# A fixed lead in the scheduler's order for the work beside a selective scan

## The chip, the cores and the metric

The kernel runs on one core of a Trainium2 chip. The metric is the device time of one execution in microseconds (us); the time given is the median of three runs. Engines are named as in the profile: PE is TensorE's matmul, PEld its weight load, DVE is VectorE, ACT ScalarE, POOL GpSimd, SP SyncE.

## What is computed

Eight images of 64 channels and 64 x 64 pixels go through four layers one after the other, all in float32:

```
x = layer0(x)   # softmax attention of all 4096 pixels over 4096, then a 3x3 depthwise and a 1x1 convolution
x = layer1(x)   # norm, then two blocks of 8x8 window attention (8 heads) and an MLP with gelu
x = layer2(x)   # a dynamic 3x3 filter made from x, leaky relu, a 1x9 convolution
x = layer3(x)   # norm, projection, depthwise conv, selective scan in 4 directions, gate, then a
                # multi-scale depthwise stage (max pools, 3x3 convolutions, gelu)
```

The selective scan is the recurrence of layer 3, for 128 channels and 16 states along 4096 positions, in four directions:

```
h = h * exp(dt_t[..., None] * A) + dt_t[..., None] * B_t[:, :, None, :] * u_t[..., None]
y_t = einsum('bkcn,bkn->bkc', h, C_t)
```

## The kernel before

Images are worked on in four pairs p = 0 to 3; the two images of a pair share the 128 partitions. The work of a pair has three parts:

- **the front** (`front(p)`): layers 0 to 2 and the sources of the scan. `layer0` is the attention: 8 column chunks by 32 row tiles by 2 images of a score matmul (L1324), an exp on ACT (L1330) and a weighing matmul (L1316), then a convolution. `layer1` is a norm, two rounds of eight window rows (L1453, L1470, L1471, L1483, L1494) and of an MLP (L1552 to L1560). `layer2` weighs nine taps on DVE (L1619) and sums them on PE (L1625, L1637). `scan_sources` normalises, projects, convolves (L1275, L1277) and stores x2, xc, xt and zs in device memory; its last instructions are the 16 z (L1693), eight for each image.
- **the scans** (`scans(p)`): 2 images x 4 directions x 8 chunks of 512 positions make 64 units of 8 steps, so 512 steps a pair and 2048 in all. A step takes two pairs of states. `fetch` loads B and C rows three and two steps ahead (four buffers each, SP's queue), `products` makes dt·u·B on POOL (L1809, eight buffers `v`), `step` makes two exps on ACT (L1831), two scans on DVE (L1834), copies the ends for the next chunk (L1838) and multiplies by C on POOL or DVE (L1842), `sums` folds the result into the accumulator `yd` on PE (L1854). Once a unit there are `load`, `inputs`, `spread` for the next and `gather` for the last one; after the last direction (the order is 1, 3, 0, 2, and the last runs from chunk 7 down to 0) `gather` stores the chunk of `ys` (L1873). The next chunk of a direction needs the carries of the one before.
- **the back** (`back(p)`): from chunk 7 down to 0 it loads x2, and for both images y (from `ys`, L1890) and z, normalises and gates (L1894, L1895: 16 `u`), projects and adds; then the multi-scale stage, and the store of the output.

`begin` runs front 0 alone. Then there are four sections. Section p traces the scans of pair p, and beside them, one after the other, back(p-1) and front(p+1); the last section has back(2), spread over more steps, and near its end back(3), which the program calls `late`. The generators yield an estimated cost, and the loop of `scans` pulls work from them in proportion to the steps, so that it is used up LEAD = 24 steps before the section's end.

The program gives every instruction a number in the order in which it is traced (a counter that goes up by one for each). The scheduler then makes each engine's queue: it goes through the program in a model of time, and gives a free engine, among the instructions of that engine which are ready, the one with the lowest number. So an instruction of the front that has fallen behind has a lower number than the scan instructions now ready, and one that is ahead has a higher. On the chip each engine works its queue in that fixed order.

The front and the back take their large tiles from three slabs (`self.slabs`, three buffers of one tag), in the order of the trace; the front's and the scans' PSUM banks are apart (`pf`, `ps`), save while the front is alone and in the last section after its back stage has been traced, when `bank` alternates between them.

Of the kernel before, what the change touches and what calls it, by code (L numbers as in the profile page):

```python
# [25 lines left out]
NTD = L // TD  # L26
GRP = 2
LEAD = 24
TC = 1024
NTC = L // TC  # L30
SLAB = 66 * 66
# [206 lines left out]
class _Net:  # L238
# [764 lines left out]
    def piece(t, k, c):  # L1003

        if k % 2 == 0:
            return t.rearrange("p (h w) -> p h w", w=64)[:, c * TC // 64 : (c + 1) * TC // 64, :]
        return t.rearrange("p (h w) -> p w h", w=64)[:, c * TC // 64 : (c + 1) * TC // 64, :]

    def scan_inputs(self, XC, unit, pools):
# [6 lines left out]
        nbc = 2 * NST  # L1016
        px = ps.tile([P, TC], F32, name="px", tag="pr")
        for h in range(TC // CH):
            nc.tensor.matmul(
# [5 lines left out]
            )  # L1025
        xd = wk.tile([nbc + RNK, TC], F32, name="xd", tag="xd", bufs=1)
        nc.scalar.activation(xd, px[0 : nbc + RNK], AF.Copy)
# [132 lines left out]
class _Direct:  # L1160
# [552 lines left out]
    def scans(self, p, beside, cost):  # L1713

        self.units = []
        for im in range(2):
            out = self.memory("ys")
            self.kept["y", 2 * p + im] = out  # L1720
            for nth, k in enumerate((1, 3, 0, 2)):
                order = range(NTD) if k < 2 else range(NTD - 1, -1, -1)
                self.units += [dict(image=2 * p + im, k=k, c=c, at=at, nth=nth, out=out) for at, c in enumerate(order)]
        self.load(self.units[0])
        self.inputs(self.units[0])
        self.spread(self.units[0])
        n = 8 * len(self.units)

        late = self.back(p) if p == B // 2 - 1 else None
        steps = [{} for _ in range(n)]  # L1730
        done = 0
        for i in range(-3, n):
            if i + 3 < n:
                self.fetch(i + 3, steps[i + 3], 0)
            if 0 <= i + 2 < n:
                self.fetch(i + 2, steps[i + 2], 1)
                self.products(i + 2, steps[i + 2])
            if i >= 0:
                self.step(i, steps[i])
                for j in self.DUE[i % 8]:  # L1740
                    if i + j >= 0:
                        self.sums(i + j, steps[i + j], steps[i]["w"])
                if i % 8 == 2 and i > 8:
                    self.gather(self.units[i // 8 - 1])
                if p == B // 2 - 1 and done >= cost:
                    self.turn = max(self.turn, 0)
                while done < cost * (i + 1) / (n - LEAD):
                    done += next(beside, cost)
            if late and i >= n - 8 * (NTD - 1) and i % 8 in (3, 5, 7):
                next(late)  # L1750
            if i >= 0 and i % 8 < 3 and i // 8 + 1 < len(self.units):
                (self.load, self.inputs, self.spread)[i % 8](self.units[i // 8 + 1])
        for i in (n - 2, n - 1):
            self.sums(i, steps[i])
        self.gather(self.units[-1])
        self.run(beside)
        if late:
            self.run(late)
# [285 lines left out]
```

## Time and profile before

| | |
|---|---|
| median of three runs | 11726.25 us (11724.63 to 11733.27) |
| the profiled execution | 11724.67 us, its span 11722.8 us |
| granted TensorE clock, mean | 0.896 |
| busy: PE, DVE, ACT, POOL | 9682.2, 8416.8, 7078.9, 6924.2 us |
| scans on DVE (L1834, the four groups) | 2602.0 + 1922.7 + 352.3 + 261.9 us, 4096 of them |
| attention exps on ACT (L1330) | 2048, 589 ns each |
| DMA | 1577.06 MB, mean 135 GB/s |

The profile is of one execution. Its page has the busy time of each engine and the busy tenths in 40 equal slices. A table of stretches gives for each stretch of time, in us from the span's start, its length, the busy time of each engine with the number of its instructions, the granted clock, the DMA engines' share and the GB/s; for one source line alone it gives those instructions only. Busy PE time is modelled, since matmuls are pipelined.

The front's stages can be told by their lines: front 0 has its attention from 45 to 579 us and its last z at 1547; front 1 has its first exp at 1579, its last at 2600, its last z at 4024; front 2 has 4437, 5388 and 6790; front 3 has 7200, 8149 and 9562. The last scan starts at 11602.8, and the output's last stores follow.

### The profile page before, as it was taken

How to read it: one execution, taken by the hardware profiler on the slowest of the kernel's cores; microseconds unless marked ns; L12 is line 12 of the kernel's file. 1: busy time of each engine (PE TensorE's matmuls, PEld its weight loads, DVE VectorE, ACT ScalarE, POOL GpSimd, SP SyncE). 2: the span in 40 equal slices, each digit the busy share in tenths (PEclk: the TensorE clock that was granted, in tenths of full speed). 3: DMA queues.
4: the chain of work that ended last, by engine and by line, in shares of the span. 5: the costliest groups of instructions: out<-in, count | busy, mean ns of one | idle time of the engine just before them, and what ended most of it. 6: DMA issues, size and time to landing. Idle time of an engine off the chain costs nothing. (4 is left out here: it accounts for less than half of the span.)

```text
span 11722.8 us, 161838 instructions
## 1 busy us (share of the span) xinstructions
PE 9682.2 (83%) x55454; PEld 3278.2 (28%) x55454; DVE 8416.8 (72%) x9856; ACT 7078.9 (60%) x16513; POOL 6924.2 (59%) x3799
## 2 busy tenths in 40 slices
PE   9987899998879779998888969999888976655556
PEld 2244332223332222222442213222333221111111
DVE  0033368887777685778777775878778669989998
ACT  5545367766664756776665665776666465555554
POOL 0000058876665565777555574777556558778994
PEclk9998989999999889999999879999998977877677
DMA  0000055553444554555333463555334356556663
GB/s 21 1 2 2 27 164 176 172 174 118 128 124 123 168 165 128 167 169 164 103 113 110 140 201 102 171 166 173 120 106 129 109 172 196 171 177 200 205 205 120
DMA packets 779781, 1577.06 MB, mean 135 GB/s; under 512 B 89280, under 2 KB 89408, under 8 KB 778176
## 3 DMA queue, kind: packets, MB, share of 16 engines
q1 hardware_dynamic: 736320, 1443.18, 40.6%
q10 hardware_dynamic: 42624, 123.44, 3.7%
q8 instruction: 438, 7.18, 0.2%
q14 instruction: 399, 3.27, 0.1%
HBM read 1197.16 MB, written 100.66 MB: 111 GB/s over the span
## 5 line engine op out<-in xcount | busy, mean ns | idle before, releaser
L1809 POOL TENSOR_TENSOR vd<-B,du 128x1024 f32<-128x1024 f32 x2048 | 4801.7, 2363 | 2896.0 <-DMA B<-rows 1732.7
L1842 POOL TENSOR_TENSOR vd<-hd,C 128x512 f32<-128x512 f32 x1737 | 2210.8, 1278 | 1765.4 <-DVE hd L1834 1719.2
L1854 PE MATMUL yd<-vd,pack 128*64 128x512 f32 x8192 | 2684.9, 691 | 602.0 <-POOL vd L1842 501.5
L1831 ACT ACTIVATE dad<-du,As 128x512 f32<-128x512 f32 x4096 | 2719.1, 682 | 635.5 <-DVE vd L1842 412.5
L1834 DVE TENSOR_TENSOR_SCAN dad<-dad,carry,vd 128x512 f32<-128x512 f32 x2064 | 2602.0, 1275 | 228.4 <-ACT dad L1831 224.8
L1834 DVE TENSOR_TENSOR_SCAN hd<-dad,carry,vd 128x512 f32<-128x512 f32 x1520 | 1922.7, 1266 | 347.5 <-ACT dad L1831 298.2
L1842 DVE TENSOR_TENSOR vd<-dad,C 128x512 f32<-128x512 f32 x2359 | 1559.6, 673 | 167.9 <-ACT carry L1838 128.7
L1324 PE MATMUL s<-X 64*128 64x512 f32 x4096 | 1542.2, 644 | 74.9 <-ACT e L1330 68.9
L1330 ACT ACTIVATE e<-s 128x512 f32<-128x512 f32 x2048 | 1197.3, 589 | 468.1 <-PE s L1324 467.8
L1854 PEld LDWEIGHTS yd<-vd,pack 128*64 128x64 f32 x8192 | 651.9, 151 | 2292.6 <-issue 1169.1
L1316 PE MATMUL po<-e,VT 128*64 128x512 f32 x4096 | 1264.5, 620 | 9.5 <-ACT e L1330 8.7
L1838 ACT ACTIVATE carry<-dad 128x1 f32<-128x1 f32 x2063 | 345.8, 169 | 903.4 <-DVE dad L1834 804.4
L1324 PEld LDWEIGHTS s<-X 64*128 64x128 f32 x4096 | 422.2, 186 | 1181.4 <-issue 831.3
L1838 ACT ACTIVATE carry<-hd 128x1 f32<-128x1 f32 x1521 | 303.1, 200 | 678.4 <-DVE hd L1834 669.8
L1483 PE MATMUL w_av<-wide,vals 64*32 64x64 f32 x16384 | 502.6, 227 | 127.3 <-DVE w_oc L1512 74.2
L1483 PEld LDWEIGHTS w_av<-wide,vals 64*32 64x32 f32 x16384 | 416.7, 113 | 258.9 <-issue 138.6
L1316 PEld LDWEIGHTS po<-e,VT 128*64 128x64 f32 x4096 | 250.5, 135 | 841.0 <-issue 565.7
L1471 ACT ACTIVATE wide<-wide 128x512 f32<-128x512 f32 x512 | 310.9, 628 | 287.0 <-DVE wide L1470 287.0
L1494 PE MATMUL w_av<-wide,each 64*32 64x128 f32 x8192 | 474.4, 284 | 8.4 <-issue 8.3
L1243 PE MATMUL pv<-n_sq,pack 128*128 128x512 f32 x576 | 354.7, 700 | 139.6 <-ACT n_sq L1241 127.0
L1771 PE MATMUL pdd<-xs,xdt 128*128 128x512 f32 x512 | 343.7, 758 | 122.3 <-DVE hd L1834 64.2
L1330 ACT ACTIVATION_READ_ACCUMULATOR e<-s 128x1 f32 x2048 | 406.7, 199 | 0.0
(258 smaller groups left out, 10839.1 us busy)
## 6 DMA issues: line engine op xcount, KB each, us to landing
B<-rows SPq DMA_DIRECT2D x2048, 256.0 KB, 3.6
C<-rows SPq DMA_DIRECT2D x2048, 256.0 KB, 3.5
du<-du SPq DMA_DIRECT2D x384, 512.0 KB, 5.5
du<-du ACTq DMA_DIRECT2D x128, 512.0 KB, 5.2
xs<-xt SPq DMA_DIRECT2D x128, 256.0 KB, 3.7
xs<-xc SPq DMA_DIRECT2D x128, 256.0 KB, 3.8
xc<-xcv ACTq DMA_DIRECT2D x64, 256.0 KB, 2.0
xt<-XT ACTq DMA_DIRECT2D x32, 512.0 KB, 5.9
```

Source lines behind the costliest of these rows:

```text
L1243: nc.tensor.matmul(pv, lhsT=avg, rhs=sq, start=True, stop=True)
L1316: nc.tensor.matmul(po[half[im]], lhsT=VT[:, t, half[im]], rhs=es[im], start=(t == 0), stop=(t == 31))
L1324: nc.tensor.matmul(ss[im], lhsT=at(half[im], t), rhs=X[half[im], jc * CH : (jc + 1) * CH], start=True, stop=True)
L1330: nc.scalar.activation(e, ss[im], AF.Exp, scale=C**-0.5, accum_out=parts[:, im, t, jc : jc + 1])
L1483: nc.tensor.matmul(self.av[rows, 0, x % 4 + j], lhsT=net.vals[half[im], x + j, 4 * g + h], rhs=es[g][half[im], j, h], tile_position=(64 * ...
L1494: nc.tensor.matmul(self.av[rows, 1, x % 4 : x % 4 + 2], lhsT=net.each[half[im], 32 - HD - HD * h : 64 - HD - HD * h], rhs=es[g][half[im], ...
L1809: self.nc.gpsimd.tensor_tensor(v, self.twice(st["B"]), self.units[i // 8]["du"][:, :, 1], ALU.mult)
L1831: nc.scalar.activation(da, u["du"][:, j, 0], AF.Exp, scale=net.As[:, k, n : n + 1])
L1834: nc.vector.tensor_tensor_scan(along(to), along(da), along(v[:, j]), first, ALU.mult, ALU.add)
L1838: nc.scalar.activation(self.carries[:, n : n + 1], ends, AF.Copy)
L1842: m = engine.tensor_tensor(v[:, j], hs[j], CC, ALU.mult)
L1854: m = nc.tensor.matmul(u["y"][self.HALF[j]], lhsT=w["fold"], rhs=st["v"][:, j], start=(i % 8 == 0), stop=(i % 8 == 7))
```

## The change

The block in which `scans` pulls work of the front and the back is put under `high_priority(offset=AHEAD)`. This sets the counter back by 600 for the instructions traced inside, and sets it to its old value afterwards, so that these instructions no longer advance the counter. No instruction is added, removed or changed; `begin`, the rest of `beside` after the loop and `late` keep their numbers.

```
+AHEAD = 600
...
                 while done < cost * (i + 1) / (n - LEAD):
-                    done += next(beside, cost)
+                    with self.tc.high_priority(offset=AHEAD):
+                        done += next(beside, cost)
```

## The prediction, made before the result was known

> **What bounds the kernel now.** I read the page's busy line and slices first, then a table of stretches cut at the front's own stages (first and last exp of L1330, last z of L1693), then the same stretches for the scan instruction L1834 alone, which counts scan steps (two scans to a step, 2048 steps in all).
>
> From the page, busy tenths in 40 slices (293 us each):
>
> ```profile
> PE   9987899998879779998888969999888976655556
> DVE  0033368887777685778777775878778669989998
> PEclk9998989999999889999999879999998977877677
> ```
>
> TensorE is high for three quarters of the span, VectorE only at the end. Stretches, all engines: the first front's attention and its rest, alone; the turn between two sections; the third front's attention beside scans; two stretches after the last front, with no front or back work:
>
> ```profile
> 45.00:579.00 534.00, 534.00 (x2042) 130.44 (x2039) 4.85 (x7) 322.95 (x1023) 0.00 (x0) 1.00 0.00 1
> 579.00:1547.00 968.00, 797.45 (x9146) 383.59 (x9144) 350.57 (x570) 433.45 (x697) 0.00 (x0) 0.90 0.06 20
> ...
> 4024.00:4437.00 413.00, 321.09 (x766) 105.82 (x767) 321.55 (x373) 219.68 (x479) 265.38 (x146) 0.86 0.52 158
> 4437.00:5388.00 951.00, 922.46 (x3014) 253.66 (x3011) 715.30 (x757) 686.62 (x1955) 691.82 (x373) 0.99 0.54 159
> ...
> 10368.00:10600.00 232.00, 125.25 (x266) 24.15 (x266) 199.66 (x212) 113.86 (x264) 192.11 (x105) 0.70 0.63 191
> 10600.00:11385.00 785.00, 445.97 (x1026) 97.11 (x1024) 746.61 (x797) 406.95 (x992) 737.45 (x400) 0.71 0.67 204
> ```
>
> The columns after the length are PE, PEld, DVE, ACT, POOL. Attention is TensorE's (534 of 534 us alone, 922 of 951 with scans); the scans alone are VectorE's (747 of 785). The same for L1834 alone, from the second front's attention on (columns: length, DVE busy with the number of scans, clock, DMA share, GB/s):
>
> ```profile
> 1579.00:2600.00 1021.00, 626.22 (x510) 0.99 0.60 176
> 2600.00:4024.00 1424.00, 577.57 (x470) 0.91 0.44 132
> 4024.00:4437.00 413.00, 188.56 (x154) 0.86 0.52 158
> 4437.00:5388.00 951.00, 525.57 (x429) 0.99 0.54 159
> 5388.00:6791.00 1403.00, 543.05 (x441) 0.90 0.41 126
> ...
> 9562.00:10368.00 806.00, 469.94 (x385) 0.78 0.59 179
> 10368.00:10600.00 232.00, 148.79 (x122) 0.70 0.63 191
> 10600.00:11385.00 785.00, 549.56 (x454) 0.71 0.67 204
> 11385.00:11622.00 237.00, 125.59 (x103) 0.83 0.58 178
> ```
>
> After the last front's end at 9562 there are 385 + 122 + 454 + 103 = 1064 scans left, 532 steps: that front ended with the scans at step 1516 of 2048. The table gives two prices of a scan step. Alone it costs 232/61 = 3.80 us, and 785/227 = 3.46 us once the scans have the front's PSUM banks too. Beside a front it costs far less: the second front's attention carried 255 steps in 1021 us and the third's 214.5 in 951, so 70 us for 40.5 steps, **1.73 us a step**; for whole fronts (2445 us with 490, 2354 with 435) it is 91/55 = 1.65. So a step moved from beside a front to a place without one costs about 2 us. Who has the right of way today is seen where the third front's attention starts (L1834 alone, 50 us each):
>
> ```profile
> 4350.00:4400.00 50.00, 10.29 (x9) 1.00 0.26 83
> 4400.00:4450.00 50.00, 4.91 (x4) 0.83 0.24 85
> 4450.00:4500.00 50.00, 2.66 (x3) 1.00 0.03 9
> 4500.00:4550.00 50.00, 32.27 (x28) 1.00 0.67 189
> ```
>
> The back stage had fallen behind the scans, so the front's instructions had the older numbers; they took TensorE, the scans fell to 1.5 steps in 50 us, and at 4500 the two were level and went on in step (14 steps). A front that is behind already goes first. What the offset adds is that it goes first until it is ahead.
>
> **The change, part by part.** Nothing is added or removed but order. One scan step issues 2 exps, 2 scans, 2 products with C (and up to 2 carries, 1.75 on average), 1 product with B, 2 matmul calls, 2 fetches: 12.75; a unit of 8 steps adds 12 to 13 (load, two matmuls, four activations, a product, row store, spread, gather), so 14.3 instructions a step. The counter is put back after the block, so front instructions do not advance it: 600 numbers are 600/14.3 = **42 scan steps**. Where front and scans compete at level today, they will compete with the front 42 steps ahead; the pattern inside a section is the same, shifted. What changes is at the ends.
>
> (1) The first section. The second front cannot start earlier: it waits for the first one's slabs and pools, as today (its first exp is at 1579, 32 us after the first front's last z). It then takes TensorE until it leads by 42 steps, as at 4400 to 4500. Its attention carries some 213 steps instead of 255: 42 x 1.73 = **-73 us** until that front's end. Bounds: 42 x 3.8 = -160 if a step cost there what it costs alone, 0 if it cost nothing.
>
> (2) The last front. It ends with the scans at about step 1474 instead of 1516. Those 42 steps still have to be done, without a front, VectorE-bound, at 3.80 us: **+160 us** (at 3.46, +145). The third back stage beside them moves forward by the same 42 steps, so its own cost stays.
>
> (3) The two turns between. The back stage needs the three slabs of the front that is ending, then, from the last chunk down, what the scans of the second image's last direction store. Today the front's last z is at 4024 with the scans at step 493 of 512, when five of the eight chunks are stored; the sixteen u (L1895) of the stage come between 4087 and 4283, at step 554. Forty-two steps earlier the front ends at step 451, chunk 7 is complete at 456 and chunk 0 only at 512: the stage is held to one chunk in 8 steps. To step 512 that is 61 steps, as many as today from z to the last u (259 us, 4.25 a step), and behind the last store come its load and one chunk's norms (4 us and 196/8 = 25 us): some 35 us longer. The 8 steps done more in the turn are missing in the next attention (8 x 1.73 = -14 us). **+20 us each, +40** for both; bounds: 0 (the stage is not held), +90 (nothing given back). VectorE and ACT have room for it there (322 and 220 of 413 us).
>
> (4) Queues. SyncE's queue carries B and C for the scans, and the moved back stage issues its loads of y into it, now just behind the stores of the same rows: store 3.5 us and load 4.3 us to landing. B and C run three steps (over 11 us) ahead, which hides 7.8 us; uncovered it would be 8 x 7.8 = 62 us a section. I take 0. ACT's queue carries xc, xt, zs and the spread of the last images: same order within the front, 0. POOL has no front work; it only starves when the scans do, as at 4400, 0 beyond (1).
>
> Sum: -73 + 160 + 40 = **+127 us**. The profiled execution took 11724.67 us (span 11722.8), 1.6 under the median of 11726.25: 11852, say **11850**.
>
> Two rules of the Trainium skill against this sum. In the stretches without a front the granted clock was 0.70 and 0.71, against 0.99 in attention, so longer such stretches mean slower matmuls; yet VectorE is the bound there and TensorE is idle 46% of the time, so I add nothing. The skill ("TensorE: Matmul & The Clock Gate", Part 1) says that the array's clock is gated until activity releases it; were TensorE on the path there, that rule would add something, which no run here prices. And its "Perfetto Trace Analysis" (Identifying the Most-Contended Engine) says that busy matmul time is no measure of headroom and weight-load time should be used: by that, 254 of 951 us, attention has room, a step costs nothing in it, term (1) is 0 and the sum +200. The 70 us for 40.5 steps decide here.
>
> **The rivals.**
> - *The fronts themselves get shorter* (the other side). Layer 2 and the sources run level with the scans today: 3556 to 4024, 468 us, against 306 us for the first front alone (1241 to 1547). The excess, some 160 us a section, 480 for three, is partly front instructions queueing behind scan ones. If precedence gave back half while the scans filled the same holes: -240 + 127, **11610**. It decides from 127/480, a quarter, on. For it: ACT and DVE are each under 70% there, so there are holes. Against: where the front was behind and already first, it went no faster than its own chain.
> - *The back stage's loads block SyncE's queue*: the uncovered price of (4) in three sections, +187 us at most, half of it likely: **11945**. For it: y's load already waits for ys 8 times today. It decides if B's wait grows in the turns.
> - *The offset does nothing*: if in the scheduler's model the fronts are rarely ready when a scan instruction is, order hardly moves: **11726**. Against: the level stretch after 4500 is a contest.
>
> **How the numbers follow.** Forecast 0.55 (own range 11750 to 11925: (1) at -120, (2) at +145, (3) at 0 for the low end; -50, +160 and +90 for the high one), SyncE 0.17, nothing 0.06, shorter fronts 0.22, spread over 11500 to 11720. A measurement of this kernel tells about 0.2%, 23 us, from no change. Range 11600 to 11980: it leaves out the better half of the shorter fronts and the worst of SyncE. Faster 0.22, same 0.06, slower 0.72.
>
> **What would show it.** Right: the second front's attention starts with 100 to 150 us of almost no scans and takes about 950 us; the last z comes near 9530 with some 1475 steps done; L1834 then has about 1146 instructions left instead of 1064; the turns show the back stage beginning before the section's last scan step and paced by stores. Wrong: the fronts' non-attention stretches shrink well below 1400 us with as many scans in them; or the step count at the last z stays near 1516.

## The result and the profile after

The changed kernel takes 12749.2 us (median of four runs, 12740.08 to 12754.33) against 11725.44 for the kernel before beside it: ratio 1.087, interval 1.085 to 1.0885. The forecast of 11850 had the side right and the size far too small, outside its range. The profiled execution has a span of 12738.3 us and a mean clock of 0.865 (0.896 before). In this program the lines from 1748 on are two higher than in the one before, those from 29 to 1747 one higher: the scan is L1836, the window scores L1454.

The page of the kernel after, busy times and tenths (now 318 us a slice):

```profile
PE 10599.9 (83%) x55454; PEld 3559.2 (28%) x55454; DVE 8425.7 (66%) x9856; ACT 7093.4 (56%) x16505; POOL 6929.5 (54%) x3799
...
PE   9977999988989789998898869998988975665556
...
DVE  0133367776566757776656685778566668988998
...
PEclk9998999988888889998878889999888887777777
```

VectorE, ScalarE and GpSimd have the busy time they had. TensorE has 918 us more with the same 55454 matmuls, nearly the 1016 by which the span grew, and its clock is lower in the middle of each front. Stretches of the kernel after, all engines: turn, third front's attention, then 232 and 785 us from the last front's end:

```profile
4232.00:4659.00 427.00, 323.61 (x756) 103.39 (x756) 321.75 (x369) 220.09 (x485) 276.09 (x155) 0.85 0.52 158
4659.00:5697.00 1038.00, 976.26 (x3010) 267.67 (x3010) 706.20 (x743) 690.19 (x1957) 689.73 (x373) 0.95 0.49 144
...
10419.00:10651.00 232.00, 138.24 (x322) 31.20 (x318) 199.94 (x213) 124.21 (x288) 201.28 (x115) 0.76 0.61 184
10651.00:11436.00 785.00, 499.52 (x1132) 126.17 (x1132) 703.24 (x752) 429.19 (x955) 621.82 (x330) 0.77 0.60 181
```

The same kernel, scan instructions alone. First the 100 us from the second front's first exp, then its attention, its windows and MLP, its layer 2 and sources, the turn, the third front's attention and its windows and MLP, and everything behind the last z:

```profile
1567.00:1617.00 50.00, 4.66 (x4) 0.99 0.27 82
1617.00:1667.00 50.00, 8.25 (x7) 1.00 0.17 42
```
```profile
1567.00:2583.00 1016.00, 529.57 (x436) 0.97 0.52 152
2583.00:3678.00 1095.00, 395.96 (x321) 0.85 0.36 106
3678.00:4232.00 554.00, 183.92 (x149) 0.86 0.41 126
4232.00:4659.00 427.00, 189.78 (x155) 0.85 0.52 158
4659.00:5697.00 1038.00, 514.99 (x423) 0.95 0.49 144
5697.00:6781.00 1084.00, 379.49 (x308) 0.82 0.34 102
...
10419.00:12738.30 2319.30, 1395.13 (x1144) 0.76 0.60 182
```

The lead is there, and of the size worked out: the attention starts with 100 us of almost no scans, and 1144 scans are left behind the last z (1146 forecast). What had not been expected is the length of the fronts. The ledger below is cut at the first and last exp of each attention, the last addition of the MLP, the last z, and the end; each entry is us / scan steps.

| part | before | after | us more |
|---|---|---|---|
| to the second front's first exp | 1579 / 4 | 1567 / 0 | -12 |
| attentions beside scans | 1021 / 254, 951 / 214, 949 / 214 | 1016 / 218, 1038 / 212, 1038 / 212 | -6, 87, 89 |
| windows and MLP | 903 / 158, 871 / 149, 878 / 149 | 1095 / 160, 1084 / 153, 1079 / 153 | 192, 213, 201 |
| layer 2 and sources | 521 / 77, 532 / 71, 535 / 71 | 554 / 74, 557 / 69, 540 / 69 | 33, 25, 5 |
| turns | 413 / 77, 409 / 78 | 427 / 78, 424 / 78 | 14, 15 |
| behind the last z | 2161 / 532 | 2319 / 572 | 158 |

The tail behind the last z costs what was forecast (+160); the second front's attention gained almost nothing of the 73 us. Windows and MLP cost 606 us more with as many scan steps in them, and 587 of that lies between the first and the last projection of the window rows (`w_pp`, with the first of the two MLP rounds between them). The third front's rows, cut there, before and then after:

```profile
5595.00:6154.00 559.00, 471.99 (x7866) 240.52 (x7864) 420.74 (x554) 364.25 (x751) 304.08 (x171) 0.95 0.37 110
```
```profile
5907.00:6675.00 768.00, 700.39 (x7886) 322.69 (x7886) 432.45 (x564) 369.42 (x772) 321.07 (x179) 0.79 0.28 83
```

The same work, 209 us longer: VectorE, ScalarE and GpSimd do nearly as much, TensorE is busy for 228 us more at 0.79 of the clock instead of 0.95. The timeline of TensorE shows why. Start, length of the run of matmuls, line and tiles; before, then after, in the same part of a window row:

```profile
5657.37 1.51 PE L1453 MATMUL w_s<-wide,w_kk 32*64 32x256 f32 x20
...
5663.43 1.09 PE L1453 MATMUL w_s<-wide,w_kk 32*64 32x256 f32 x14
5664.45 0.43 PE L1483 MATMUL w_av<-wide,vals 64*32 64x64 f32 x16
5664.69 0.40 PE L1494 MATMUL w_av<-wide,each 64*32 64x128 f32 x8
5664.91 0.40 PE L1483 MATMUL w_av<-wide,vals 64*32 64x64 f32 x16
5665.14 0.40 PE L1494 MATMUL w_av<-wide,each 64*32 64x128 f32 x8
```
```profile
6053.10 0.64 PE L1454 MATMUL w_s<-wide,w_kk 32*64 32x256 f32 x2
6053.67 0.30 PE L1484 MATMUL w_av<-wide,vals 64*32 64x64 f32 x2
6053.90 0.64 PE L1454 MATMUL w_s<-wide,w_kk 32*64 32x256 f32 x2
6054.47 0.30 PE L1484 MATMUL w_av<-wide,vals 64*32 64x64 f32 x2
6054.69 0.64 PE L1454 MATMUL w_s<-wide,w_kk 32*64 32x256 f32 x2
```

Before, scores (`w_s`, 32 rows of the array) and weighings (`w_av`, 64 rows) go mostly in large groups. After, in many stretches, they alternate two by two (a float32 matmul of the code stands in the trace as two: 4096 scores for the code's 2048, so it is one matmul of each kind in turn), and each round of four matmuls takes 0.80 us (6053.10 to 6053.90). At the pace of the rows before, two scores are 2 x 0.06 us (20 in 1.51 us, the last one 0.37) and two weighings 2 x 0.015 (16 started in 0.24): 0.15 us. Over the whole trace, in order of start, TensorE goes directly from one of the two kinds to the other 342 times before and 1252 times after. Two groups of the page of the kernel after belong to it: the scores, busy for 798.5 us (344.0 before), and VectorE's idle time ahead of the bias, 449.9 us (109.8 before), nearly all of it put down to a weighing:

```profile
L1454 PE MATMUL w_s<-wide,w_kk 32*64 32x256 f32 x4096 | 798.5, 456 | 28.4 <-DVE wide L1471 26.5
...
L1471 DVE TENSOR_TENSOR wide<-w_s,bias 128x512 f32<-128x512 f32 x512 | 328.4, 683 | 449.9 <-PE w_av L1495 379.1
```

This is not the front against the scans, it is the front against itself. The counter is put back after each block that is pulled, so the next block starts from a number that is higher only by what the scans issued in between. A scan step issues some 14 instructions, a block of the window attention some 60 (8 scores, 48 weighings, two biases, two exps). By the trace of the kernel before, the third front issues about 34 a scan step in windows and MLP (5019 in 148.5 steps, matmuls counted as in the code) and 7 in its attention (1539 in 214.5). So in the window rows several successive blocks of the front share a range of numbers, and a score of a later block can have the number of an earlier block's weighing; in the attention, by this count, only blocks pulled at one step do. That gives the theory: *the front's own order is lost (1), and the lead has little to do with it*. The rival: *the lead itself does it (2)*, since scans and front meet at other places.

### The profile page after: what moved, and what is told of

It is laid out like the page before. It is cut to its first block, busy times and chain, and to the rows that moved or that the text cites. A ratio compares the mean times of both kernels' runs of the same rounds, so it can differ in the third digit from the quotient of the medians.

```text
span 12738.3 us, 161752 instructions
## 1 busy us (share of the span) xinstructions
PE 10599.9 (83%) x55454; PEld 3559.2 (28%) x55454; DVE 8425.7 (66%) x9856; ACT 7093.4 (56%) x16505; POOL 6929.5 (54%) x3799
## 5 line engine op out<-in xcount | busy, mean ns | idle before, releaser
L1811 POOL TENSOR_TENSOR vd<-B,du 128x1024 f32<-128x1024 f32 x2048 | 4796.7, 2360 | 3562.2 <-DMA B<-rows 1829.8
L1856 PE MATMUL yd<-vd,pack 128*64 128x512 f32 x8192 | 2896.7, 703 | 686.9 <-POOL vd L1844 612.7
L1836 DVE TENSOR_TENSOR_SCAN dad<-dad,carry,vd 128x512 f32<-128x512 f32 x2064 | 2600.5, 1275 | 85.2 <-ACT dad L1833 82.5
L1836 DVE TENSOR_TENSOR_SCAN hd<-dad,carry,vd 128x512 f32<-128x512 f32 x1520 | 1925.0, 1267 | 160.5 <-ACT dad L1833 120.0
L1325 PE MATMUL s<-X 64*128 64x512 f32 x4096 | 1511.1, 654 | 164.9 <-ACT e L1331 136.4
L1856 PEld LDWEIGHTS yd<-vd,pack 128*64 128x64 f32 x8192 | 677.7, 154 | 2554.1 <-issue 1198.6
L1317 PE MATMUL po<-e,VT 128*64 128x512 f32 x4096 | 1326.0, 641 | 15.0 <-ACT e L1331 12.8
L1454 PE MATMUL w_s<-wide,w_kk 32*64 32x256 f32 x4096 | 798.5, 456 | 28.4 <-DVE wide L1471 26.5
L1484 PE MATMUL w_av<-wide,vals 64*32 64x64 f32 x16384 | 669.3, 241 | 46.1 <-ACT wide L1472 22.9
L1471 DVE TENSOR_TENSOR wide<-w_s,bias 128x512 f32<-128x512 f32 x512 | 328.4, 683 | 449.9 <-PE w_av L1495 379.1
L1484 PEld LDWEIGHTS w_av<-wide,vals 64*32 64x32 f32 x16384 | 498.0, 121 | 404.5 <-issue 307.7
L1495 PE MATMUL w_av<-wide,each 64*32 64x128 f32 x8192 | 582.7, 308 | 2.1 <-issue 2.0
```

Of the source, the lines that this page charges most:

```text
L1317: nc.tensor.matmul(po[half[im]], lhsT=VT[:, t, half[im]], rhs=es[im], start=(t == 0), stop=(t == 31))
L1325: nc.tensor.matmul(ss[im], lhsT=at(half[im], t), rhs=X[half[im], jc * CH : (jc + 1) * CH], start=True, stop=True)
L1454: nc.tensor.matmul(ss[g][half[im], j], lhsT=K[rows, 64 * (x + j) : 64 * (x + j) + 64], rhs=qx[rows, x + j], start=True, stop=True,)
L1484: nc.tensor.matmul(self.av[rows, 0, x % 4 + j], lhsT=net.vals[half[im], x + j, 4 * g + h], rhs=es[g][half[im], j, h], tile_position=(64 * ...
L1495: nc.tensor.matmul(self.av[rows, 1, x % 4 : x % 4 + 2], lhsT=net.each[half[im], 32 - HD - HD * h : 64 - HD - HD * h], rhs=es[g][half[im], ...
L1811: self.nc.gpsimd.tensor_tensor(v, self.twice(st["B"]), self.units[i // 8]["du"][:, :, 1], ALU.mult)
```

## Experiments

e2, e5, e8c and e10 were run once each, e1, e7, e8 and e11 four times, e12 five times.

**The counter put back, without a lead** (`e2_put_back_no_lead`). The change with its offset at nought:

```
-AHEAD = 600
+AHEAD = 0
```

> Offset 0: no lead, but the counter is put back after each block as in the changed kernel. Theory 1 (own order): most of the loss is there without any lead, 12750 - 127 = 12620 us (12450 to 12750), third front's window rows 740 to 790 us, last z at scan step 1516. Theory 2 (precedence): the same as before, 11726 us (11690 to 11790), window rows 560 us.

Measured 12518.65 us, 798 over the kernel before and inside the range of the first theory. Turns (407, 404), tail (2157) and the scan step at the last z are those of the kernel before, so there is no lead; its window rows (780, 756, 755 us) are those of the change. The third front's:

```profile
5917.00:6673.00 756.00, 688.28 (x7878) 317.84 (x7880) 436.77 (x570) 372.13 (x772) 318.28 (x179) 0.82 0.28 84
```

Scores and weighings change over 1281 times. The rival (2) is out for the windows: putting the counter back is enough. Attentions 2 and 3 are 54 and 56 us longer too, which their 216 steps (214 before) don't explain.

**The window's order tied, in the changed kernel** (`e5_window_order`). Each score matmul is held behind the last weighing traced before it and the reverse, as an order on TensorE alone, without a semaphore (shortened; `last_s` and `last_av` are the last matmul traced of each kind):

```
     m = nc.tensor.matmul(            # the scores, L1454
...
+    if self.last_av is not None:
+        net.behind(m, self.last_av)
...
     m = nc.tensor.matmul(            # both weighings, L1484 and L1495
...
+    net.behind(m, self.last_s)
```

> The changed kernel, but on TensorE alone the score matmuls (w_s) and the weighing matmuls (w_av) of the window rows are tied to their traced order; every other engine and everything else as in the changed kernel. Theory 1, with the cost in TensorE's alternation between the two kinds: window rows from 765 to 560-600 us in each of three sections, 12750 - 3 x 190 = 12180 us (12080 to 12260), the attention's 1038 us stay. Theory 1, with the cost on other engines (VectorE and ScalarE waiting for buffers in mixed order): 12600 us or more. Theory 2: 12750 us.

Measured 12215.59 us, 534 less than the change, with the lead kept; the first theory had forecast 12080 to 12260. The third front's window rows, with the clock back at 0.94:

```profile
5749.00:6325.00 576.00, 487.52 (x7892) 240.78 (x7890) 426.95 (x558) 369.12 (x768) 314.53 (x177) 0.94 0.36 109
```

Window rows 615, 576 and 579 us, 299 changes instead of 1252. Two readings of what one costs: parts of windows and MLP, 1095 + 1084 + 1079 less 931 + 892 + 896, are 539 us for 953 changes, 0.57 us each; all start-to-start times of these two kinds in the trace, 1551 us after and 961 here, give 0.62. The dense rows above give (0.80 - 0.15) / 2 = 0.33; the rest is waiting that the alternation brings, and the clock, which no run took apart. The order within the window rows is shown to be their cause. The attentions stay at 1038.

**A lead with the counter going on** (`e1_lead_in_order`). The block starts 1020 numbers back, and what it issues advances the counter:

```
-                    with self.tc.high_priority(offset=AHEAD):
-                        done += next(beside, cost)
+                    at = self.tc.cur_priority
+                    with self.tc.high_priority(offset=AHEAD):
+                        done += next(beside, cost)
+                        at = self.tc.cur_priority + AHEAD
+                    self.tc.cur_priority = at
```

> The front keeps a lead of the same 42 scan steps (offset 1020, the counter goes on after the block, so that the front's instructions have numbers of their own and stand in their own order). Theory 1 (own order: the counter that is put back gives successive blocks of the front the same numbers, so that their instructions are mixed): what is left is the shift that the prediction priced, 11850 us (11790 to 11910), the third front's window rows (first w_h to last w_pp) back at 560 to 600 us with 0.9 granted clock or more. Theory 2 (precedence: the scans are starved and TensorE's clock falls, because the front goes first): over 12500 us, window rows near 760 us.

Measured 12066.39 us, ratio 1.029 (1.027 to 1.031); 216 over the expectation. Scores and weighings change over 333 times, as before, but the window rows are 674, 652 and 654 us. They hold more scans: windows and MLP 179 steps in 974 us instead of 149 in 871, the sources 49 in 493 instead of 71 in 532. In window rows the front issues many numbers a step, so a lead of 1020 numbers is fewer steps there. The steps that moved cost 3.4 us each (103 us for 30) where they came and gave back 1.8 (39 for 22) where they left. A fixed distance in numbers is no fixed distance in steps, and this run is no clean test of the sum.

**The same lead in steps, numbers set by hand** (`e8_lead_42_grid`; `e8c_lead_0_grid` with AHEAD = 0). Each scan step gets 256 numbers, the front's go 42 steps back and never below the last one it used:

```
+        base = self.tc.cur_priority + 3 * GRID
...
+            self.tc.cur_priority = base + GRID * i
...
+                at = self.tc.cur_priority
+                self.tc.cur_priority = max(base + GRID * (i - AHEAD) + GRID // 2, self.next_front)
                 while done < cost * (i + 1) / (n - LEAD):
                     done += next(beside, cost)
+                self.next_front = self.tc.cur_priority
+                self.tc.cur_priority = at
```

> A constant lead: the numbers are set by hand, 256 to a scan step; the front's instructions traced at step i get numbers half-way in step i - 42, one after the other and never lower than the front's last one. So the lead is 42 steps in every stage (a fixed offset in instructions is shorter in the window rows, where the front traces many) and the front's own order is kept. Shift theory (the prediction's sum is right once the front's order is left alone): 11850 us (11800 to 11890), third front's attention 937 us and its window rows 560. Rival (a lead itself makes the shared stages slower, as the fixed lead's attention of 976 us hints): 12000 us or more, attention 970 or more.

> Control: the same numbering by hand with a lead of 0. Both theories: as before, 11721 us (11690 to 11760). If it is far from that, the numbering by hand has an effect of its own, and the run with the lead of 42 is to be read against this one.

Measured 11829.0 us, ratio 1.0087 (1.007 to 1.0104), and 11793.89 for the one without a lead, outside the 11690 to 11760 expected of it. The first is the case that the prediction's sum describes: lead of 42, order kept, 451 steps done at the second front's end and 574 left behind the last z. Its second front's attention and its third window rows:

```profile
1576.00:2535.00 959.00, 896.68 (x3004) 237.73 (x3003) 723.33 (x764) 691.90 (x1981) 711.45 (x384) 0.95 0.55 161
...
5569.00:6127.00 558.00, 472.44 (x7870) 239.00 (x7866) 419.48 (x551) 362.44 (x754) 305.95 (x171) 0.94 0.36 110
```

The window rows are short again with the lead in place. The third front's attention, 967 us, missed the 937 expected and came near the rival's 970. The control shows a price of the numbering itself: 69 us, with attentions of 1048, 978 and 978 us instead of 1021, 951 and 949 at the same steps. So the long attentions of e8 go with the numbering and not with the lead, and against the control the lead of 42 costs 35 us.

Put beside the changed kernel, which ends its fronts at nearly the same steps, e8 gives a price of the lost order, with the price of its own numbering in it. The spans differ by 905 us: windows and MLP 620, attentions 201, layer 2 and sources 108, the rest -24.

**The counter put back once a step** (`e10_put_back_once_a_step`). The blocks of one step keep their order among themselves:

```
+AHEAD = 0
...
-                while done < cost * (i + 1) / (n - LEAD):
-                    done += next(beside, cost)
+                with self.tc.high_priority(offset=AHEAD):
+                    while done < cost * (i + 1) / (n - LEAD):
+                        done += next(beside, cost)
```

> Offset 0 and the counter put back, but once a scan step instead of once a block: the two blocks of attention that are traced at one step no longer share numbers. If sharing numbers within a step is what made the attention slower (1005 us against 951 with the same steps), it is back at 951 to 960, the window rows, where one block alone has more instructions than a scan step, stay at 740 to 760: 12519 - 3 x 50 = 12370 us. If the attention's loss has another cause, it stays at 1005 and the time near 12520.

Measured 12405.13 us. Window rows stay at 764, 757 and 754 us with 1285 changes: blocks of neighbouring steps still overlap. The attentions come to 991 us, not to 951: numbers shared within a step make 14 of the 54 us in e2. A miss, and where the other 40 come from stays open.

**The other direction** (`e7_lead_0`, `e11_lead_minus_24`). If a lead costs at the ends, less of the distance LEAD, by which `scans` uses up its work ahead of the section's end, should pay:

```
-LEAD = 24
+LEAD = 0
```

and in the second `LEAD = -24`.

> The kernel before with LEAD = 0 instead of 24: the other direction, the front is spread over all 512 steps of a section. By the two prices of a scan step (1.73 us beside attention, 3.8 alone): 20 steps more beside fronts, 20 fewer after the last one, 11726 + 35 - 76 = 11685 us (11640 to 11720). If instead the next section's scans then wait for their sources at the turns: 11750 us or more.

> The kernel before with LEAD = -24: a twentieth of a section's front is left over when the scans have been traced, and is traced before the next section. By the prices of a step, if the chip overlaps it with the next section's scans: some 20 steps more beside the fronts than with LEAD = 0 (11623 us), another 40 to 90 us less, 11535 to 11585 us. If the next section's scans wait for their sources: 11650 us or more.

LEAD = 0: 11623.07 us, ratio 0.9914 (0.9898 to 0.9931), a gain of 98 us, better than expected. The turns are 353 us with 65 steps instead of 413 with 77, and 512 steps instead of 532 are left behind the last z (2091 us instead of 2161, 3.5 a step). The attention pays for it: 268 steps in 1066 us instead of 254 in 1021, 3.4 us for each step more, twice the 1.73 of the expectation. LEAD = -24: 11654.74, ratio 0.9942, faster than before but slower than LEAD = 0. Its front outlasts the section. The scans of the section run out at step 512 while it still has its sources to make; this is the scan line in the 80 us ahead of the second front's first z:

```profile
3899.00:3979.00 80.00, 9.95 (x9) 1.00 0.11 40
```

Nine scans in 80 us: the front runs nearly alone there, and GpSimd waits 100 us in one piece for the next pair's first rows of B, which need the sources. So the second case of the expectation came in, at its bound of 11650 us: the next section's scans wait for their sources.

**LEAD = 0 with the window's order tied** (`e12_lead_0_window_order`). Both edits shown above, in the kernel before.

> The kernel before with LEAD 0 and, beside it, every score matmul of the window attention held behind the weighing matmuls traced before it and the other way round, so that TensorE changes between the two less often. In the program as scheduled that leaves 281 changes instead of 329 with LEAD 0 alone. If a change between the two shapes costs 0.55 to 0.62 us, as the runs with 940 to 950 changes more gave, 48 fewer are worth 26 to 30 us: 11595 against 11623 for LEAD 0 alone, with the window rows at about 550 us each instead of 560 to 590. If the cost was in the large mixing only (the queue far from its traced order) and not in each change, the time stays at 11623.

Measured 11624.44 us, ratio 0.9913 (0.9899 to 0.9927), the same as LEAD = 0 alone. The gain of 26 to 30 us did not come. The changes between the two kinds fell from 329 to 281 in the trace, but the start-to-start times of both kinds in all stayed (969 and 967 us): the steps from one kind to the other took 15 us less (150 to 135), and TensorE's idle time between matmuls of one kind grew by 19 us (62 to 81). What was saved at the changes came back as waiting. The price of 0.6 us is not a price for every change; these runs show it where the order is lost and some 950 changes come on top. No version that was run is faster than LEAD = 0 alone.

## Why the prediction was right and wrong

**The failed step** is the sentence that ended the derivation of the lead: "the pattern inside a section is the same, shifted. What changes is at the ends." It treated the offset as a shift of the front against the scans. The text even said that front instructions no longer advance the counter, and drew from it only the size of the lead (600/14.3). The same fact compresses the front's own numbers: what goes on by 14.3 a step while the front issues some 34 in windows and MLP must overlap itself. No term stood for it. What the runs showed in its place: most of the loss is there without any lead (+798 us in e2), 534 of the change's 1024 us go when the order of the window rows alone is tied (e5), and with a lead of 42 steps and the order kept (e8) the span is 905 us shorter than the changed kernel's. The timeline of the kernel before held a hint: large groups of scores, then of 16 and 8 weighings in turn, are something that the numbers produced and that could be lost.

The terms of the sum, each with the change itself and with e8, where the order is kept (in brackets e8 against its control without a lead):

| term | predicted | change | e8 |
|---|---|---|---|
| (1) second front's attention | -73 | -6 | -62 (-89) |
| (2) behind the last z | +160 | +158 | +149 (+149) |
| (3) each turn | +35 | +14, +15 | +22, +31 (+29, +32) |
| (3) given back in each next attention | -14 | +87, +89 | +16, +15 (-11, -13) |
| sum, with all else | +127 | +1015 | +110 (+41) |

- **Size of the lead.** Right: 452 steps at the second front's last z (451 forecast), 1476 at the last front's (1474).
- **Term (1).** Right in kind where the order is kept, not settled in size. In e8 some 37 steps left, not 42: 62 us, 1.7 us a step, against the kernel before, but 89 us, 2.4 a step, against the control, by which e8 was to be read; with LEAD = 0 the steps that came cost 3.4. So the 1.73, worked out from two sections of one run, is no fixed price; the 0 that the prediction set beside it from weight-load time is out. In the change the same 37 steps left and nothing was gained, since the mixed attention took as much as the scans had. The forecast "takes about 950 us" came out at 1016.
- **Term (2).** Right: 40 steps for 158 us, 3.95 each against 3.80; in e8 42 for 149, 3.55 each.
- **Term (3).** Right in cause: the 16 `u` of the second section's back stage lie between steps 466 and 514, eight steps to a chunk, as the stores come. The +20 of the sum is 35 us longer less 14 given back, but the text's own pieces, 4 and 25 us, add to 29. In the change a turn took 14 and 15 us and one scan step more, not eight; in e8 it took nine steps more (86) and 22 and 31 us. What it gives back shows only against the control.
- **The sum in e8.** That +110 is so near +127 is partly luck. Against the control the lead costs +41. The terms make some 97 of that (-89 + 149 + 29 + 32 - 11 - 13); against them stand 54 us for which the sum had nothing: windows and MLP 12 us shorter in all, layer 2 and sources 35, the second front's start 7 earlier.
- **Term (4), queues.** The idle time of POOL that ends with B's arrival went from 1732.7 to 1829.8 us, with tails and windows that are longer by far more; the turns, where the *SyncE rival* had its price, are 14 us longer and not 60. It is out.
- *The fronts get shorter*: the opposite happened, and e8 settles why it could not decide. With the order kept and the lead in place, windows and MLP take 898, 875 and 865 us instead of 903, 871 and 878, and the sources 525, 512 and 506 instead of 521, 532 and 535: some 60 us for three sections (47 against the control), not the 240 of the rival's sum. Precedence over the scans is worth little there.
- *The offset does nothing*: out.

**What stays open.** The attentions lose 54 to 56 us in e2, 87 to 89 in the change, 27 to 29 in the control e8c, in each case with nearly the scan steps of before. TensorE changes between its three kinds of work there about as often (847 and 851 times in the third front's attention, before and after), so it is not the number of changes. In e2 the loss stands in one place: in the third front's attention the steps from one weighing matmul to the next take 180 us instead of 126, nearly as many of them (687 and 680), and the others balance out. TensorE's idle time that ends with an exp, ahead of a weighing, is 32 us there instead of 3.5, so weighings come up there before their exps are done. In the changed kernel the loss is spread (weighings 27 us, scores 25, the scans' matmuls 11), and what links it to the numbers is not known. The 108 us in layer 2 and the sources have no cause shown either.

## What to carry to other kernels

A priority that is lent to a block and taken back is a plain shift only if the blocks after it get higher numbers than it has; ask first whether a stage that is pulled in pieces keeps its own order, by comparing what the pieces issue with what the counter gains between two of them. Price a shift at its ends, but look at the rows in between for an order that the numbers had made by chance. And where a sum finds that having work ahead costs, the other direction is worth a run: it was where the gain lay, up to the point where the work that is behind outlasts what it should run beside.

## What the runs showed of the hardware

Matmuls of two shapes that take turns two by two are far dearer than the same matmuls in groups: 0.80 us for four against 0.15 us. The rows show two parts of this. The last score ahead of a change starts 0.31 us before the weighing, in both kernels (5664.14 to 5664.45, and 6053.36 to 6053.67). But before, 14 scores and that change take 1.02 us together (5663.43 to 5664.45), 0.07 us each, while after, the second score of a pair starts 0.26 us behind the first (6053.10 to 6053.36). So the alternation pays for more changes, and it also loses the overlap that scores have in a group; no run takes the two apart. The Trainium skill ("TensorEngine Tiling (Array Packing)", Tiling Modes, Key Properties) says that a change of the tiling mode drains TensorE, where a change of tile doesn't; scores use 32 rows by 64 columns of the array, weighings 64 by 32, and the 0.31 us at a change fit that. The skill gives no time for it, no run here prices it alone, and in e12 fewer changes brought nothing.

The granted clock in the window rows fell to 0.79 with TensorE busy 91% of the time, and was 0.95 with it busy 84%; with the order tied it is 0.94 again. More busy time thus went with a lower clock. The skill's page on the clock gate ("TensorE: Matmul & The Clock Gate", Part 1) has idle windows lower the clock; busy time by the profile is modelled here and may include time in which the array stands still, so the two need not clash, but no run shows which it was.
